# A graph layer's gathers: 45 tiles of rows move from the SP queue's single-row loads to POOL's indirect loads

## The chip, the cores and the metric

The kernel runs on one core of one Trainium2 chip. A core has five engines, each with an instruction queue of its own: TensorE (PE, matrix products; PEld is its weight load), VectorE (DVE), ScalarE (ACT), GpSimd (POOL) and SyncE (SP, which here issues transfers only). Sixteen DMA engines move data between device memory and the core's on-chip memory. The metric is the device time of one execution in microseconds (us).

## The reference

400,000 edges, sorted by destination, connect 12,500 nodes of 48 features. Each edge has 32 attributes. The layer is

```python
h = maximum(layernorm(x), 0)
tmp = concatenate([h[dst], h[src], edge_attr], axis=1)     # 400000 x 128
msg = relu(tmp @ W1 + b1) @ W2 + b2
out = x + segment_sum(msg, dst, num_segments=12500)
```

with W1 of 128 x 128 and W2 of 128 x 48, all float32.

## The kernel before

**Tables.** `tmp @ W1` splits into three products: one of the destination node, one of the source node, one of the edge. A first part of the kernel (about 135 us) computes for every node a row of 128 numbers for its use as destination (`tab_a`, bias included) and one for its use as source (`tab_b`), and writes both tables to device memory. The source table is also kept on chip, transposed, as `bt` (128 partitions, one column for each node).

**Chunks and steps.** The edges go in 3,125 tiles of P = 128 edges, and in NCH = 391 chunks of T = 8 tiles (the last has five). The loop at the end of `windows` takes one chunk further in each of 393 steps, in an order written out by hand: step c loads chunk c (`prepare`), multiplies chunk c-1 (`before`, `turned`, `hidden`) and sums chunk c-2 (`fold`, `add`). Because the edges are sorted, the 1,024 edges of a chunk point to a window of at most W = 80 destination nodes.

- `prepare(c)` has SP issue three loads: `rhs`, the 80 rows of `tab_a` that belong to the window (line 362; three buffers in turn), the edge attributes into the lower part of `lhs` (line 367), and the destinations, repeated over 80 partitions, into `row` (line 369). `lhs` and `row` have three buffers each. POOL issues the indirect loads of line 376: one for each tile, each fetching 128 rows of `tab_b` of 512 bytes into a slot of `gb`. There are six `gb` buffers, so the gathers of chunk c wait until line 420 has read chunk c-6. DVE compares `row` with the window's numbers (line 383) and builds the one-hot matrix `hot` (line 388).
- `before(c-1)` has PE compute `pre`, the destination part and the edge part in one product (line 401).
- `hidden(c-1)` has DVE add the gathered source rows `gb` to `pre` (line 420); ACT applies the relu (lines 424 and 425).
- `fold(c-2)` and `add(c-2)` sum a chunk's edges into its window by a product with `hot` (lines 433 and 438), and DVE adds that to a segment of 1,024 nodes (line 452) at a place that comes from a register.
- Every GQ = 12 chunks the segment changes (`segment_next`: lines 468 and 470). A finished segment is multiplied by W2 (lines 478 and 479), added to its part of x (line 480) and stored (line 484). SP issues the load of that part of x (line 461) and the store.

**Three ways to fetch source rows.** Most tiles are fetched by POOL's indirect loads. Two sets of tiles are not.

- `BYCOLS`, 361 chunks: the last tile of the chunk is copied out of `bt` on chip, one column of 128 x 1 for each edge, by DVE (59 columns in a step) and ACT (60) at line 353. Each copy has its place from a register; `load` fills these registers (line 304, TENSOR_LOAD). PE turns the finished tile and adds it to `pre` (line 411). The parts of a step's columns are spread over the step: 23, 20 and 16 on DVE and 28 and 32 on ACT.
- `BYROWS`, 45 chunks: one more tile of the chunk is fetched by SP, row by row, RPART = 15 rows in each step (`rows`, line 322), into a tile `gs` of its own. Each row takes a register number (sixteen of them in SP's load of line 304: the window's place and fifteen rows), a move and an issue. Line 420 then adds one tile less, and line 422 adds `gs` to the last one.

`last` is the table of these numbers, `WIDTH` = 140 for each step: up to 119 columns, the window's place at `BASE` = 120, fifteen rows, and four numbers for segments. A tile that is in neither set, or only in one, counts with POOL: `range(n - (c in BYCOLS) - (c in BYROWS))`, thus mostly seven gathers for a chunk, six where both sets have it, eight where none has.

Of the kernel before, what the change touches and what calls it, by code (L numbers as in the profile page):

```python
# [8 lines left out]
F32 = mybir.dt.float32  # L9
# [7 lines left out]
P = 128  # L17
N, D, DE, HID, E = 12500, 48, 32, 128, 400000
# [4 lines left out]
T = 8  # L23
# [20 lines left out]
U8 = mybir.dt.uint8  # L44
# [3 lines left out]


COLS = 1  # L50
ROWS0 = 1
END = NT // T


# [3 lines left out]
)  # L58
PART = sum(n for _, _, n, _ in PARTS)
BASE = 120  # L60
RPART = 15

BT0 = 16512
SEG0 = 122144
SEG_SIZE = 8 * L


SEG, NEXT, SEG2 = 136, 137, 138
PLACE0 = 139
WIDTH = 140  # L70
SLOTS = (NCH + 2 + P - 1) // P
MOST = 32

# [1 line left out]
def tiles_of(first, part):  # L75

    n = (END - first) * part // P
    return [first + (P * (j + 1) + part - 1) // part - 1 for j in range(n)]


BYCOLS = tiles_of(COLS, PART)
BYROWS = tiles_of(ROWS0, RPART)
EPS = 1e-5


# [149 lines left out]
def windows(nc, tc, gp, bt, ident, idx, x_t, tab_a, tab_b, dst, edge_t, w1, w2s, b2s, out_t):  # L235
# [3 lines left out]
    with ExitStack() as es:  # L239
# [5 lines left out]
        gtp = es.enter_context(tc.tile_pool(name="gtp", bufs=3))  # L245
# [13 lines left out]
        for _, _, n, at in PARTS:  # L259
# [1 line left out]
                last[:, :, at : at + n], last[:, :, at : at + n], 4, BT0,  # L261
                op0=ALU.mult, op1=ALU.add,
            )
        rows_at = slice(BASE, BASE + 1 + RPART)
        nc.vector.tensor_scalar(
            last[:, :, rows_at], last[:, :, rows_at], 4 * HID, None, op0=ALU.mult
        )
        tab8, taba8 = (t.rearrange("n h -> (n h)").bitcast(U8) for t in (tab_b, tab_a))

        place = PARTS[0][3] - 1  # L270
        for a, b in ((place, SEG2), (NEXT, SEG)):
# [5 lines left out]
        nc.vector.scalar_tensor_tensor(  # L277
            last[:, :, at_place], last[:, :, at_place], 4.0, last[:, :, PLACE0 : PLACE0 + 1],
            op0=ALU.mult, op1=ALU.add,
# [8 lines left out]
            rhss.append(rhs)  # L288
        st = {}
        gts = {}  # L290
        gss = {}

        def group(c):

            return divmod(c + OFF, GQ)
# [4 lines left out]
        def numbers(c, at, n, engine):  # L300

            got = []
            for k in range(0, n, MOST):
                got += nc.values_load_multi_w_load_instructions(  # L304
                    last[c % P : c % P + 1, c // P, at + k : at + min(k + MOST, n)],
                    engines=[engine], min_val=0, max_val=1 << 23,
                    skip_runtime_bounds_check_because="numbers of nodes, and what is made of them",
                )[1]
            return got

        def node(n):
            return n.with_bounds(min_val=0, max_val=N - 1)

        def rows(c, nodes):

            for k, n in enumerate(nodes):
                e = (c - ROWS0) * RPART + k
                of = BYROWS[e // P]
                if of not in gss:
                    gss[of] = gtp.tile([P, HID], F32, name="gs")  # L320
                n = n.with_bounds(min_val=0, max_val=4 * HID * (N - 1))
                nc.sync.dma_start(  # L322
                    gss[of].bitcast(U8)[e % P : e % P + 1, :],
                    tab8[bass.ds(n, 4 * HID)].rearrange("(o h) -> o h", o=1),
                )

        regs = {}

# [12 lines left out]
        def columns(c, part):  # L341

            dve, first, _, _ = PARTS[part]
            copy = nc.vector.tensor_copy if dve else nc.scalar.copy
            for k, at in enumerate(regs.pop((c, part), [])):
                j, e = divmod((c - COLS) * PART + first + k, P)
                of = BYCOLS[j]
                if of not in gts:
                    gts[of] = gtp.tile([HID, P], F32, name="gt")
                at = at.with_bounds(  # L350
                    min_val=BT0, max_val=BT0 + 4 * (N - 1), guaranteed_mod_val=0, out_of_modulus=4
                ) - BT0
                copy(gts[of][:, e : e + 1], bt8[:, bass.ds(at, 4)].bitcast(F32))  # L353

        def prepare(c):
            n = min(T, NT - c * T)
            at = c * CE
            m = max(0, min(RPART, len(BYROWS) * P - (c - ROWS0) * RPART)) if c >= ROWS0 else 0
            base, *nodes = numbers(c, BASE, 1 + m, mybir.EngineType.SP)
            rhs = rhss[c % 3]  # L360
            base = base.with_bounds(min_val=0, max_val=4 * HID * (N - 1))
            nc.sync.dma_start(
                rhs.bitcast(U8)[:W, :],
                taba8[bass.ds(base, 4 * HID * W)].rearrange("(w h) -> w h", w=W),
            )
            lhs = ld.tile([P, CE], F32, name="lhs")
            nc.sync.dma_start(lhs[W:K, : n * P], edge_t[:, at : at + n * P])
            row = ld.tile([W, CE], I16, name="row")
            nc.sync.dma_start(
                row[:, : n * P],  # L370
                dst[at : at + n * P].rearrange("(o e) -> o e", o=1).to_broadcast([W, n * P]),
            )
            st[c] = dict(n=n, rows=nodes)
            gb = gp.tile([P, T, HID], F32, name="gb")
            for t in range(n - (c in BYCOLS) - (c in BYROWS)):
                nc.gpsimd.indirect_dma_start(  # L376
                    out=gb[:, t, :], out_offset=None, in_=tab_b[:, :],
                    in_offset=bass.IndirectOffsetOnAxis(
                        ap=srci[:, c * T + t : c * T + t + 1], axis=0
                    ),  # L380
                )

            nc.vector.tensor_scalar(  # L383
                lhs[:W, : n * P], row[:, : n * P], bw[:, c : c + 1], None, op0=ALU.is_equal,
            )
            columns(c, 0)
            hot = wp.tile([P, T, W], F32, name="hot")
            nc.vector.tensor_tensor(  # L388
                hot[:, :n, :], wnum.unsqueeze(1).to_broadcast([P, n, W]),
                rel[:, c * T : c * T + n].unsqueeze(2).to_broadcast([P, n, W]), op=ALU.is_equal,  # L390
            )
            load(c, 1)
            st[c].update(rhs=rhs, lhs=lhs, gb=gb, hot=hot)
# [21 lines left out]
        def hidden(c):  # L415
            s = st[c]
            n, m, pre = s["n"], s["added"], s["pre"]
            h = wp.tile([P, T, HID], F32, name="hid")
            g = m - (c in BYROWS)
            nc.vector.tensor_add(h[:, :g, :], pre[:, :g, :], s["gb"][:, :g, :])  # L420
            if g < m:
                nc.vector.tensor_add(h[:, g, :], pre[:, g, :], gss.pop(c))
            if m < n:
                nc.scalar.activation(h[:, m, :], pre[:, m, :], AF.Relu)  # L424
            nc.scalar.activation(h[:, :m, :], h[:, :m, :], AF.Relu)  # L425
            s["h"] = h
# [16 lines left out]
        def add(c):  # L443

            s = st.pop(c)
            k = group(c)[0] % 2
            of = SEG0 + k * SEG_SIZE
            at = s["base"].with_bounds(
# [33 lines left out]
        def segment_store(g, n):  # L482
            first, = numbers(begin(g), SEG, 1, mybir.EngineType.SP)
            nc.sync.dma_start(out_t[:, bass.ds(node(first), n)], xs.pop(g)[:, :n])

        with tc.manual_schedule():
            for c in range(NCH + 2):
                if c < NCH:
                    prepare(c)
                    rows(c, st[c].pop("rows"))  # L490
                if c >= NCH:
                    columns(c, 0)
                columns(c, 1)
                load(c, 2)
                columns(c, 2)
                if 0 <= c - 1 < NCH:
                    before(c - 1)
                if 0 <= c - 2 < NCH:
                    fold(c - 2)
                if 0 <= c - 1 < NCH:  # L500
                    turned(c - 1)

                g, k = group(c - 2)
                if k == GQ - 3 or c == NCH - 1:
                    segment_load(g)
                if g > 0 and k < L // BLK:
                    segment_sum(g - 1, k, BLK)
                if g > 0 and k == STORE:
                    segment_store(g - 1, L)
                columns(c, 3)  # L510
                if 0 <= c - 1 < NCH:
                    hidden(c - 1)
                load(c + 1, 0)
                load(c, 4)
                columns(c, 4)
                if 0 <= c - 2 < NCH:
                    add(c - 2)
                    if k == GQ - 1:
                        segment_next(g)
                load(c + 1, 3)  # L520
                if c == NCH + 1:
                    segment_sum(g, 0, END_L)
                    segment_store(g, END_L)

                if c < PIECES:
                    s = slice(c * PIECE, (c + 1) * PIECE)
                    nc.sync.dma_start(out_t[:, s], x_t[:, s])
# [126 lines left out]
def tile_gnn_preln(  # L654
# [52 lines left out]
    flag = const.tile([1, 1], I32, name="flag")  # L707
    last = const.tile([P, SLOTS, WIDTH], I32, name="last")

# [157 lines left out]
```

## Time and profile before

| | |
|---|---|
| median of 3 runs | 5028.71 us (5015.86 to 5036.02) |
| the profiled execution | 5046.97 us |
| its span, first to last instruction | 5045.2 us |
| busy: PE, PEld | 3196.2 us (63%), 2891.6 us (57%) |
| busy: DVE, ACT, POOL | 2915.2 us (58%), 2927.7 us (58%), 2664.5 us (53%) |
| mean granted TensorE clock | 0.643 of full speed |
| DMA: software queue (POOL), hardware queue (SP, ACT) | 178.39 MB, 169.09 MB |
| mean DMA rate | 70 GB/s |

A group row reads: line, engine, operation, tiles written and read, shapes, count | busy time and mean duration of one in ns | idle time of the engine just before them, and what ended most of it ("issue" where the profile knows of nothing that the engine waited for). A row of the order of time reads: start, duration, engine, line, operation, and how many of a kind follow each other without a gap, with the idle time ahead in brackets; "SPq" is SP's queue, whose transfers are shown by their issue. A row of a stretch reads: from and to, length, and for each engine the busy time and, in brackets, the count; then the granted clock, the share of DMA time and GB/s. A row of the waits reads: who waited, for what, how long in total, how often, the longest.

### The profile page before, as it was taken

The numbers are of one execution on the slowest core, as the hardware profiler recorded it, in microseconds if no ns is written. First come the engines' busy times: TensorE is split into PE (matmuls) and PEld (weight loads), VectorE is DVE, ScalarE is ACT, GpSimd is POOL, SyncE is SP. The second block draws the span as 40 slices with busy tenths as digits, with TensorE's granted clock in tenths as the row PEclk, the third lists the DMA queues.
The fourth block names the chain that finished last, engine by engine and source line by source line (L and its number), as shares of the span: only waits on it lengthen the run. The fifth ranks groups of instructions, "written<-read, shape, count | busy, mean of one in ns | idle before, by whom it ended". The sixth has DMA issues, their size and how long they took to land. (4 is left out here: it accounts for less than half of the span.)

```text
span 5045.2 us, 105760 instructions
## 1 busy us (share of the span) xinstructions
PE 3196.2 (63%) x16917; PEld 2891.6 (57%) x16917; DVE 2915.2 (58%) x24786; ACT 2927.7 (58%) x24107; POOL 2664.5 (53%) x2746
## 2 busy tenths in 40 slices
PE   6565666665666665566666665666666666666676
PEld 4555555555555555556565555556555565555565
DVE  4555555555555555565555555555555565555555
ACT  3455655655555555566565555556565566555555
POOL 5455555555555555555555555555555555555553
PEclk8666666666666666666666666666666666665656
DMA  3422222222222222222222222222222222222221
GB/s 135 123 67 69 68 66 68 68 67 68 64 65 66 68 70 67 64 68 71 67 69 69 68 67 67 69 67 69 67 67 68 69 71 68 68 66 69 66 69 51
DMA packets 202255, 354.44 MB, mean 70 GB/s; under 512 B 70322, under 2 KB 108228, under 8 KB 200276
## 3 DMA queue, kind: packets, MB, share of 16 engines
q0 software_dynamic: 87040, 178.39, 14.2%
q1 hardware_dynamic: 114256, 169.09, 11.3%
q14 instruction: 560, 4.59, 0.3%
q8 instruction: 139, 2.28, 0.2%
q10 hardware_dynamic: 260, 0.10, 0.0%
HBM read 327.84 MB, written 22.07 MB: 69 GB/s over the span
## 5 line engine op out<-in xcount | busy, mean ns | idle before, releaser
L376 POOL DMA_INDIRECT gb<-tab_b,srci x2719 | 2643.0, 972 | 2315.4 <-DVE hid L420 1319.5
L353 ACT COPY gt<-bt 128x1 f32 x23280 | 2477.9, 189 | 1893.8 <-issue 1867.1
L353 DVE COPY gt<-bt 128x1 f32 x22928 | 1704.1, 143 | 1795.4 <-issue 1750.0
L433 PE MATMUL p_g<-hot,hid 128*128 128x80 f32 x6250 | 1392.9, 414 | 1664.1 <-ACT hid L425 1585.3
L433 PEld LDWEIGHTS p_g<-hot,hid 128*128 128x128 f32 x6250 | 1313.3, 320 | 1745.7 <-ACT hid L425 1689.4
L401 PEld LDWEIGHTS pre<-rhs,lhs 112*128 112x128 f32 x6250 | 1149.6, 283 | 92.8 <-issue 85.4
L401 PE MATMUL pre<-rhs,lhs 112*128 112x128 f32 x6250 | 1171.3, 366 | 17.1 <-DVE lhs L383 17.1
L420 DVE TENSOR_TENSOR hid<-pre,gb 128x896 f32<-128x896 f32 (+2 forms) x391 | 420.8, 1076 | 6.8 <-issue 4.4
L425 ACT ACTIVATE hid<-hid 128x896 f32<-128x896 f32 (+1 forms) x391 | 370.8, 948 | 39.3 <-DVE hid L420 38.0
L411 PE MATMUL pre<-ident,gt 128*128 128x128 f32 x722 | 278.7, 489 | 112.0 <-remote 104.9
L388 DVE TENSOR_TENSOR hot<-wnum,rel 128x640 f32<-128x640 f32 x391 | 315.9, 808 | 5.1 <-issue 4.9
L383 DVE TENSOR_SCALAR lhs<-row,bw 80x1024 f32<-80x1024 int16 x391 | 306.8, 785 | 12.8 <-DMA row<-in_dst 7.9
L438 PEld LDWEIGHTS <-ones 128*128 128x128 bf16 x3125 | 291.9, 154 | 0.0
L438 PE MATMUL p_g<-hot,ones 128*128 128x80 bf16 x3125 | 283.7, 265 | 0.0
L411 PEld LDWEIGHTS pre<-ident,gt 128*128 128x128 f32 x722 | 193.4, 328 | 118.4 <-remote 110.6
L452 DVE TENSOR_TENSOR seg<-seg,p_g 128x160 f32 x391 | 125.7, 321 | 191.8 <-DVE hid L420 156.8
L424 ACT ACTIVATE hid<-pre 128x128 f32<-128x128 f32 x361 | 97.5, 270 | 86.8 <-DVE hid L420 78.4
L478 PE MATMUL p_f<-seg,w2s 128*48 128x512 f32 (+1 forms) x134 | 121.0, 1005 | 0.4 <-DVE seg L452 0.4
L479 PE MATMUL p_f<-seg,b2s 1*48 1x512 f32 (+1 forms) x134 | 95.5, 801 | 0.0
L479 PEld LDWEIGHTS p_f<-seg,b2s 1*48 1x48 f32 x134 | 13.1, 143 | 100.8 <-issue 100.8
L468 DVE MEMSET seg<- 128x944 f32 x64 | 54.1, 845 | 9.5 <-issue 0.3
L480 DVE TENSOR_TENSOR xseg<-xseg,p_f 48x512 f32<-48x512 f32 (+1 forms) x67 | 44.8, 668 | 23.3 <-PE p_f L479 22.4
(67 smaller groups left out, 306.3 us busy)
## 6 DMA issues: line engine op xcount, KB each, us to landing
gs<-tab_b SPq DMA_DIRECT2D x5760, 0.5 KB
row<-in_dst SPq DMA_DIRECT2D x390, 160.0 KB
lhs<-in_edge_t SPq DMA_DIRECT2D x390, 128.0 KB
gb<-tab_b,srci POOLq DMA_INDIRECT x2719
rhs<-tab_a SPq DMA_DIRECT2D x391, 40.0 KB
xseg<-in_x_t SPq DMA_DIRECT2D x33, 192.0 KB
out_x<-xseg SPq DMA_DIRECT2D x33, 192.0 KB
tab_b<-tab SPq DMA_DIRECT2D x3, 1280.0 KB
```

Source lines behind the costliest of these rows:

```text
L353: copy(gts[of][:, e : e + 1], bt8[:, bass.ds(at, 4)].bitcast(F32))
L376: nc.gpsimd.indirect_dma_start(out=gb[:, t, :], out_offset=None, in_=tab_b[:, :], in_offset=bass.IndirectOffsetOnAxis(ap=srci[:, c * T + t ...
L383: nc.vector.tensor_scalar(lhs[:W, : n * P], row[:, : n * P], bw[:, c : c + 1], None, op0=ALU.is_equal,)
L388: nc.vector.tensor_tensor(hot[:, :n, :], wnum.unsqueeze(1).to_broadcast([P, n, W]), rel[:, c * T : c * T + n].unsqueeze(2).to_broadcast([P ...
L401: nc.tensor.matmul(pre[:, t, :], s["lhs"][:K, t * P : (t + 1) * P], s["rhs"][:K, :], start=True, stop=c not in BYCOLS or t < n - 1,)
L411: nc.tensor.matmul(s["pre"][:, s["n"] - 1, :], gts.pop(c), ident, start=False, stop=True)
L420: nc.vector.tensor_add(h[:, :g, :], pre[:, :g, :], s["gb"][:, :g, :])
L425: nc.scalar.activation(h[:, :m, :], h[:, :m, :], AF.Relu)
L433: nc.tensor.matmul(p_g[:, 0, :], s["h"][:, t, :], s["hot"][:, t, :], start=t == 0, stop=t == n - 1)
L438: nc.tensor.matmul(p_g[:, 1, :], ones, high[:, t, 1::2], start=t == 0, stop=t == n - 1)
L452: nc.vector.tensor_add(to, to, s["p_g"])
L478: nc.tensor.matmul(p_f[:, :n], w2s, seg[:, 0, s], start=True, stop=False)
```

## The change

The set `BYROWS` and all that serves it go. Its 45 tiles are fetched as the others are, by one more indirect load of POOL each, into a slot of `gb`; line 420 adds all gathered tiles of a chunk at once and line 422 goes. SP's register load holds one number, and what SP issues for a chunk are the three loads of `prepare`. The number table shrinks from 140 to 125 columns, and with it the fixed SBUF place of the segments moves by 224 bytes. Sizes, buffers and the order of all else stay.

```diff
-ROWS0 = 1
...
-RPART = 15
...
-SEG0 = 122144
+SEG0 = 121920
...
-SEG, NEXT, SEG2 = 136, 137, 138
-PLACE0 = 139
-WIDTH = 140
+SEG, NEXT, SEG2 = 121, 122, 123
+PLACE0 = 124
+WIDTH = 125
...
-BYROWS = tiles_of(ROWS0, RPART)
...
-        rows_at = slice(BASE, BASE + 1 + RPART)
+        rows_at = slice(BASE, BASE + 1)
...
-        def rows(c, nodes):
-
-            for k, n in enumerate(nodes):
-                e = (c - ROWS0) * RPART + k
-                of = BYROWS[e // P]
-                if of not in gss:
-                    gss[of] = gtp.tile([P, HID], F32, name="gs")
-                n = n.with_bounds(min_val=0, max_val=4 * HID * (N - 1))
-                nc.sync.dma_start(
-                    gss[of].bitcast(U8)[e % P : e % P + 1, :],
-                    tab8[bass.ds(n, 4 * HID)].rearrange("(o h) -> o h", o=1),
-                )
...
         def prepare(c):
             n = min(T, NT - c * T)
             at = c * CE
-            m = max(0, min(RPART, len(BYROWS) * P - (c - ROWS0) * RPART)) if c >= ROWS0 else 0
-            base, *nodes = numbers(c, BASE, 1 + m, mybir.EngineType.SP)
+            base, = numbers(c, BASE, 1, mybir.EngineType.SP)
...
-            for t in range(n - (c in BYCOLS) - (c in BYROWS)):
+            for t in range(n - (c in BYCOLS)):
                 nc.gpsimd.indirect_dma_start(
...
-            g = m - (c in BYROWS)
-            nc.vector.tensor_add(h[:, :g, :], pre[:, :g, :], s["gb"][:, :g, :])
-            if g < m:
-                nc.vector.tensor_add(h[:, g, :], pre[:, g, :], gss.pop(c))
+            nc.vector.tensor_add(h[:, :m, :], pre[:, :m, :], s["gb"][:, :m, :])
...
                 if c < NCH:
                     prepare(c)
-                    rows(c, st[c].pop("rows"))
```

More of the change, by code (lines that the diff above doesn't have):

```diff
@@ L267, in windows @@
         )
-        tab8, taba8 = (t.rearrange("n h -> (n h)").bitcast(U8) for t in (tab_b, tab_a))
+        taba8 = tab_a.rearrange("n h -> (n h)").bitcast(U8)
         place = PARTS[0][3] - 1
@@ L290, in windows @@
         gts = {}
-        gss = {}
         def group(c):
@@ L372, in prepare @@
             )
-            st[c] = dict(n=n, rows=nodes)
+            st[c] = dict(n=n)
             gb = gp.tile([P, T, HID], F32, name="gb")
-            for t in range(n - (c in BYCOLS) - (c in BYROWS)):
+            for t in range(n - (c in BYCOLS)):
                 nc.gpsimd.indirect_dma_start(
@@ L827 @@
         numbers[COLS : COLS + len(cols), at : at + n] = cols[:, k : k + n]
-    in_rows = np.array(BYROWS) * T + T - 1 - np.isin(BYROWS, BYCOLS)
-    rows = by_tile[in_rows].reshape(-1)
-    rows = np.pad(rows, (0, -len(rows) % RPART)).reshape(-1, RPART)
-    numbers[ROWS0 : ROWS0 + len(rows), BASE + 1 : BASE + 1 + RPART] = rows
     last = np.ascontiguousarray(numbers.reshape(SLOTS, P, WIDTH).transpose(1, 0, 2))
```

## The prediction

> **What bounds the kernel now.** I read the page first, then the groups by line with shapes kept apart, the waits, and last the order of time inside single steps.
>
> ```profile
> span 5045.2 us, 105760 instructions
> ...
> L376 POOL DMA_INDIRECT gb<-tab_b,srci x2719 | 2643.0, 972 | 2315.4 <-DVE hid L420 1319.5 <-issue 710.5 <-DVE hid L422 165.9
> L353 DVE COPY gt<-bt 128x1 f32 x22928 | 1704.1, 143 | 1795.4 <-issue 1750.0 <-DMA gb<-tab_b,srci 1.7
> L420 DVE TENSOR_TENSOR hid<-pre,gb 128x896 f32<-128x896 f32 x328 | 355.1, 1083 | 6.0 <-issue 4.4 <-PE pre L411 0.6
> L420 DVE TENSOR_TENSOR hid<-pre,gb 128x768 f32<-128x768 f32 x39 | 37.0, 948 | 0.8 <-PE pre L411 0.7
> L422 DVE TENSOR_TENSOR hid<-pre,gs 128x128 f32<-128x128 f32 x45 | 12.6, 280 | 0.0
> ```
>
> No engine is busy for much over 60% of the span. POOL's idle time ends on the addition of line 420, which frees a gb buffer; DVE loses 1750 us ahead of its single-column copies, where the profile knows no releaser. The step, from one addition of line 420 to the next, shows how the two belong together:
>
> ```profile
> core 0: us, PE busy (x) PEld busy (x) DVE busy (x) ACT busy (x) POOL busy (x), PEclk, DMA share, GB/s
> 919.16:931.20 12.04, 7.54 (x42) 7.35 (x42) 7.12 (x65) 7.12 (x60) 6.97 (x7) 0.72 0.32 84
> 943.62:954.28 10.66, 7.21 (x42) 7.02 (x42) 6.75 (x65) 6.86 (x59) 5.95 (x6) 0.68 0.26 71
> 981.50:994.80 13.30, 7.13 (x42) 6.94 (x42) 7.01 (x64) 7.29 (x60) 8.07 (x8) 0.68 0.30 83
> 968.71:981.50 12.79, 8.95 (x51) 5.86 (x49) 7.62 (x66) 6.06 (x48) 6.62 (x7) 0.84 0.24 63
> 1279.30:1291.54 12.24, 11.86 (x46) 8.07 (x45) 7.80 (x65) 5.89 (x47) 6.62 (x7) 0.50 0.15 40
> 1434.36:1446.55 12.19, 10.23 (x48) 6.93 (x47) 7.73 (x65) 6.05 (x50) 6.62 (x7) 0.61 0.15 39
> 4957.07:4969.55 12.48, 8.19 (x42) 7.96 (x42) 6.91 (x64) 7.74 (x69) 6.82 (x7) 0.60 0.35 93
> 4969.55:4981.66 12.11, 5.52 (x35) 5.08 (x34) 6.84 (x65) 7.52 (x65) 6.89 (x7) 0.64 0.30 83
> 5000.29:5007.87 7.58, 5.87 (x54) 5.48 (x53) 6.47 (x65) 6.50 (x61) 0.00 (x0) 0.99 0.14 40
> ```
>
> The length of a step follows POOL's count: 10.66 us with six gathers, 12.04 with seven, 13.30 with eight, and 7.58 once POOL has nothing left, although DVE and ACT do the same work. Of the 391 additions
>
> ```profile
> 158.51 1.22 DVE L420 TENSOR_TENSOR hid<-pre,gb 128x1024 f32<-128x1024 f32 x1
> ...
> 5032.55 0.81 DVE L420 TENSOR_TENSOR hid<-pre,gb 128x640 f32<-128x640 f32 x1
> ```
>
> I take the 379 steps between the fourth (196.25) and the one at 4957.07: 39 with six gathers last 11.38 us on average, 319 with seven 12.63, 21 with eight 13.64. So POOL waits for DVE, and DVE crawls while POOL gathers. How it crawls:
>
> ```profile
> 975.74 0.22 DVE L353 COPY gt<-bt 128x1 f32 x2 [1.20 <-issue]
> 976.46 0.15 DVE L353 COPY gt<-bt 128x1 f32 x1 [0.51 <-issue]
> ...
> 980.05 0.94 DVE L353 COPY gt<-bt 128x1 f32 x14 [0.55 <-issue]
> ```
>
> ```profile
> 975.73 0.28 ACT L353 COPY gt<-bt 128x1 f32 x2 [1.13 <-issue]
> ```
>
> DVE gets one or two copies through at a time, 0.72 us apart (975.74, 976.46), and ACT gets its own at the same instant (975.73). The release comes at 980.05, 1.54 us after POOL's seventh gather ended (row below: 977.56 + 0.95). Then DVE runs off fourteen copies and line 420 follows.
>
> ```profile
> 977.56 0.95 POOL L376 DMA_INDIRECT gb<-tab_b,srci  x1 [0.31 <-issue]
> ```
>
> SP works through it as well: fifteen single rows, here from 971.04, last 9.97 us, 0.66 each, where the seven from 4955.24, at the end of a crawl, took 0.39 each.
>
> ```profile
> 971.04 9.97 SPq L322 DMA_DIRECT2D gs<-tab_b  x15
> ...
> 1269.80 8.32 SPq L322 DMA_DIRECT2D gs<-tab_b  x15
> ...
> 1291.64 0.35 SPq L484 DMA_DIRECT2D out_x<-xseg  x1
> ...
> 4955.24 2.73 SPq L322 DMA_DIRECT2D gs<-tab_b  x7
> ```
>
> **The change part by part.** *Gathers added.* Each of the 45 tiles that SP filled row by row (45 x 128 = 5760 issues) becomes one more DMA_INDIRECT on POOL: 2764 for 2719. Each costs 0.95 us and the 0.30 us of issue behind it. Cover would have to come from POOL's 1319.5 us of waiting for line 420; but that wait is the other half of the loop, not slack. Of the 45, 39 make a six into a seven (12.63 - 11.38 = 1.25 us each, 49 us) and six a seven into an eight (13.64 - 12.63 = 1.01, 6 us). Sum +55 us. If POOL's wait covered them after all, they would cost 0; the averages speak against it.
>
> *The second addition removed.* Line 422 goes 45 times, and line 420 is 128x896 where it was 128x768. Busy time: 948 + 280 - 1083 = 145 ns, 6.5 us in all; the two overlap in the pipeline, so between 0 and -6.5; I take -3.
>
> *SP's rows removed.* 5760 issues, as many register moves, and fifteen of sixteen numbers in each of SP's register loads. The transfers only change queues, since the gathers fetch the same 5760 rows. SP itself was not late:
>
> ```profile
> DVE lhs L383 <- DMA row<-in_dst: 7.9, 1, 7.9
> ```
>
> is all that DVE ever waited for SP's loads by name, so SP's own time is worth nothing on the path. What may be worth something is the beat. In seven steps with seven gathers SP issued no row while the copies crawled: five times it stood in its queue for a store (from 1278.12 to 1291.64 in the rows above, and the like four more times), and twice its rows were at an end (after 4957.97). Copies within 4.00 to 11.24 us of the step (stretch, its length, busy time and count on DVE, the same on ACT, granted clock, DMA share and GB/s):
>
> ```profile
> 972.71:979.95 7.24, 1.99 (x22) 2.73 (x23) 0.76 0.23 59
> 1283.30:1290.54 7.24, 2.72 (x31) 3.16 (x29) 0.50 0.21 55
> 1438.36:1445.60 7.24, 2.78 (x35) 3.38 (x33) 0.63 0.21 57
> 4961.55:4968.79 7.24, 1.95 (x24) 2.86 (x26) 0.50 0.41 106
> 4973.55:4980.79 7.24, 1.98 (x25) 3.56 (x31) 0.50 0.27 76
> ```
>
> The first row is a step with SP at work (22 copies on DVE), the others have SP at rest. Over all seven (the first is the step 1279.30, the last 4969.55) the mean is 29.9, over the 314 others with seven gathers 25.0. Per crawl the three queues look like sharers of one supply: without SP, the other two get more. 4.9 copies at 0.06 us (fourteen in 0.94 us at 980.05, the 0.14 of a last one taken off, thirteen steps) are 0.29 us, which no longer follow the release. The lengths agree: 12.31 us over the seven, 12.63 over all 319, a gain of 0.32. But five of the seven are of one kind, the step after a change of segment, which had no loads in flight either; the two others (12.48, 12.11) stand 0.09 us below the 12.39 that the 263 steps away from the change average. The ends are thus 0.09 and, if every step shrank to the 12.19 to 12.24 of the rest steps, 0.42 us. I take 0.24, three quarters of 0.32, nearer to the counts than to the two last rows because counts and beat show the same sharing in both kinds: 379 x 0.24 = -91 us (ends -34 and -159).
>
> *The rest.* Shorter index table, SBUF places moved, first loads not behind rows: within the 7.9 us above, taken as 0.
>
> Sum: +55 - 3 - 91 = -39 us. The profiled execution took 5046.97 us (span 5045.2 and 1.8 around it), 18.3 above the median of 5028.71; -39 makes it 5008, and against the median **4990 us**.
>
> **The rivals.** *Nothing is returned (slower).* The copies crawl because POOL gathers, whoever else issues; then +55 - 3 = +52 us, 5081. For it: the two steps at 4957 and 4969, SP silent, are barely shorter, and their 24 and 25 copies are the ordinary 25.0. Against it: 31 and 35. It decides as soon as the return is under 52 / 379 = 0.137 us a step, and it sits in the 45 steps that gain a gather. [...]
>
> *All steps fall to the rest length.* 0.42 us a step: +55 - 3 - 159 = -107, 4922. For it: five steps within 0.54 us of each other. Against it: those had no loads moving (DMA share 0.15 against 0.24), and the changed kernel keeps the three loads.
>
> *The change does not do what it says*, because SP's order still holds segment loads and stores: SP stands at the store of line 484 as now,
>
> ```profile
> SPq L484 <- DVE xseg L480: 117.8, 24, 27.8
> ```
>
> with loads two steps ahead. That is no loss; it only makes more of the steps at rest, and goes with the forecast, 4990.
>
> **How the numbers follow.** Forecast (return of 0.15 to 0.36 a step) 0.55, own range 4945 to 5025; nothing or too little returned 0.31; full return 0.14. The range reaches to the two rivals: 4910 to 5085. A measurement of this kernel tells about 0.5% (25 us) from no change. Faster by more needs a return over 0.2 us: two thirds of the forecast and all of the full return, 0.50. Within 0.5%: the rest of the forecast, 0.17. Slower: 0.33.
>
> **What would show it.** Steps with seven gathers at about 12.39 us on average, where they were 12.63 (more of them near 12.1), and 28 or more copies in the 7.24 us window: the sharing is right. No steps with six gathers, 27 with eight at about 13.4: the price of a gather is right. DVE's idle time before line 353 falls from 1750 us to about 1715 (55 more for the gathers, 91 less). Wrong: seven-gather steps still at 12.5 to 12.6 with 25 copies (then 5081), or POOL's waiting down by 57 us with the span unchanged (then the gathers were covered).

## The result, and the profile after

| | before | changed |
|---|---|---|
| median of 4 runs each | 5032.36 us (5015.86 to 5038.81) | 6382.51 us (6382.25 to 6383.16) |
| span of the profiled execution | 5045.2 us | 6380.5 us |

The changed kernel takes 1.269 times as long (95% interval 1.266 to 1.272). The forecast was 4990 us.

The page of the changed kernel: the span, the busy tenths in 40 slices of it, and the groups that answer to those shown of before.

```profile
span 6380.5 us, 94216 instructions
...
PE 3296.0 (52%) x16917; PEld 2966.1 (46%) x16917; DVE 2786.1 (44%) x24741; ACT 2783.2 (44%) x24107; POOL 2686.2 (42%) x2791
...
DVE  4555556655533333333333333333333333333333
ACT  3556655566533333333333333333333333333333
...
L358 POOL DMA_INDIRECT gb<-tab_b,srci x2764 | 2664.7, 964 | 3599.0 <-DVE hid L401 2845.5
L336 ACT COPY gt<-bt 128x1 f32 x23280 | 2338.1, 187 | 3418.5 <-issue 3400.3
...
L336 DVE COPY gt<-bt 128x1 f32 x22928 | 1569.6, 142 | 2245.3 <-issue 2213.9
...
L431 DVE TENSOR_TENSOR seg<-seg,p_g 128x160 f32 x391 | 125.7, 322 | 1211.6 <-issue 1143.9
L401 DVE TENSOR_TENSOR hid<-pre,gb 128x896 f32<-128x896 f32 (+1 forms) x391 | 426.3, 1090 | 3.1 <-issue 1.2
```

Line numbers have moved: the gathers are line 358 now, the column copies 336, the addition that ends a step 401, the sum into the segment 431, the register loads 300. Apart from PE and PEld, whose clock was lower for most of the span (0.59 in the second stretch below), and POOL with its 45 gathers, no engine is busy for longer than before. DVE's copies lose 2245.3 us where they lost 1795.4, DVE loses another 1211.6 us ahead of line 431 where it was 191.8 ahead of line 452 (row below, of before), and POOL waits 2845.5 us for line 401 where it was 1319.5 for line 420. And the slices change once: up to the eleventh of 40 (1755 us) DVE and ACT are busy for five or six tenths, from there on for three to the end.

```profile
L452 DVE TENSOR_TENSOR seg<-seg,p_g 128x160 f32 x391 | 125.7, 321 | 191.8 <-DVE hid L420 156.8
```

The additions that end a step, counted in two stretches of each kernel (from and to, length, busy time and count, then clock, DMA share and GB/s). Before:

```profile
core 0: us, DVE busy (x), PEclk, DMA share, GB/s
196.00:1749.50 1553.50, 132.34 (x123) 0.64 0.25 68
1749.50:4957.00 3207.50, 275.47 (x256) 0.64 0.26 68
```

After:

```profile
core 0: us, DVE busy (x), PEclk, DMA share, GB/s
195.00:1716.90 1521.90, 134.06 (x123) 0.64 0.26 68
1717.00:6293.00 4576.00, 282.34 (x259) 0.59 0.18 48
```

The same first 123 steps take 1521.9 us in place of 1553.5: 12.37 a step, where before had 12.63. The changed kernel is 32 us ahead at 1717 us. Then a step takes 4576 / 259 = 17.67 us, where before has 3207.5 / 256 = 12.53. From there to the end the changed kernel needs 6380.5 - 1717.0 = 4663.5 us, before 5045.2 - 1749.5 = 3295.7: 1368 us lost, against 32 won.

The order of time on DVE around that point, in the changed kernel (in brackets the idle time ahead):

```profile
1713.34 0.28 DVE L336 COPY gt<-bt 128x1 f32 x3 [1.16 <-issue]
1714.08 0.15 DVE L336 COPY gt<-bt 128x1 f32 x1 [0.46 <-issue]
...
1717.02 1.08 DVE L401 TENSOR_TENSOR hid<-pre,gb 128x896 f32<-128x896 f32 x1
1723.15 0.32 DVE L431 TENSOR_TENSOR seg<-seg,p_g 128x160 f32 x1 [5.05 <-issue]
...
1724.05 1.67 DVE L336 COPY gt<-bt 128x1 f32 x23
...
1729.48 1.30 DVE L336 COPY gt<-bt 128x1 f32 x20 [2.42 <-issue]
1733.77 1.06 DVE L336 COPY gt<-bt 128x1 f32 x16 [2.99 <-issue]
1734.75 1.08 DVE L401 TENSOR_TENSOR hid<-pre,gb 128x896 f32<-128x896 f32 x1
```

Up to 1717 the crawl is there, one to three copies at a time. After it the copies run in whole parts of 23, 20 and 16, each at one go, and the idle time stands ahead of the parts. What stands ahead of a part is its register load: one of 4.50 us starts at 1724.89 and ends 0.09 us ahead of the twenty copies at 1729.48. The loads of line 300 (instances, then shortest, median and longest in ns), first between 300 and 1700 us, then between 1800 and 6300:

```profile
L300 DVEq TENSOR_LOAD <-last x349: 307/1382/2380, 301.0 to 1696.0; - x175
L300 ACTq TENSOR_LOAD <-last x227: 1717/1911/2454, 299.6 to 1697.0; - x114
L300 SPq TENSOR_LOAD <-last x131: 267/275/478, 307.0 to 1691.5; - x131
...
L300 DVEq TENSOR_LOAD <-last x784: 309/4618/6312, 1799.5 to 6299.1; - x196
L300 ACTq TENSOR_LOAD <-last x509: 5954/6261/7164, 1798.4 to 6297.5; - x170
L300 SPq TENSOR_LOAD <-last x298: 262/273/480, 1800.2 to 6299.5; - x149
```

The same loads of the same numbers of registers take 3.3 times as long. DVE's three loads of a step have 24 (the 23 columns of the first part and the place in the segment), 20 and 16 registers, so its median is a load of 20: 69 ns a register, then 231. SP's load of one register stays at some 0.27 us, although its place in blocks 1 to 3 is no multiple of 16 bytes either. In before, the loads of this second stretch are the short ones:

```profile
L304 DVEq TENSOR_LOAD <-last x764: 307/1382/2095, 1798.9 to 4898.1; - x191
```

What changes at that step is the place of the numbers. `last` holds step c in partition c mod 128 at block c div 128, and a block is `WIDTH` numbers of 4 bytes. With 140 the blocks begin at 0, 560, 1120 and 1680 bytes, multiples of 16 all; with 125 at 0, 500, 1000 and 1500, of which only the first is one. The parts begin at numbers 0, 24, 44, 60 and 88 of a block, at multiples of 16 bytes in themselves. Block 1 begins with step 128, whose loads run ahead of its sums, just where the time jumps.

### The profile page after: what moved, and what is told of

Its sections match the earlier page's. It is cut to its first block, busy times and chain, and to the rows that moved or that the text cites. A ratio compares the mean times of both kernels' runs of the same rounds, so it can differ in the third digit from the quotient of the medians.

```text
span 6380.5 us, 94216 instructions
## 1 busy us (share of the span) xinstructions
PE 3296.0 (52%) x16917; PEld 2966.1 (46%) x16917; DVE 2786.1 (44%) x24741; ACT 2783.2 (44%) x24107; POOL 2686.2 (42%) x2791
## 4 chain that ended last, share of the span: by engine, by line
issue 53%; DVE 32%; POOL 6%; DVEq 4%; PE 2%; ACT 2%; another core or an unknown queue 1%; DMA 1%; SPq 0%; ACTq 0%; POOLq 0%
DVE gt L336 18%; POOL gb L358 6%; DVE hid L401 5%; DVE lhs L365 4%; DVEq L300 4%; DVE hot L370 4%; ACT gt L336 1%; DVE seg L431 1%; PE p_n L178 1%; PE p_g L412 0%; DVE seg L447 0%; DVE xseg L459 0%; PE p_n L199 0%; PE pre L383 0%
## 5 line engine op out<-in xcount | busy, mean ns | idle before, releaser
L358 POOL DMA_INDIRECT gb<-tab_b,srci x2764 | 2664.7, 964 | 3599.0 <-DVE hid L401 2845.5
L336 ACT COPY gt<-bt 128x1 f32 x23280 | 2338.1, 187 | 3418.5 <-issue 3400.3
L412 PE MATMUL p_g<-hot,hid 128*128 128x80 f32 x6250 | 1426.1, 422 | 2810.3 <-ACT hid L404 2650.3
L412 PEld LDWEIGHTS p_g<-hot,hid 128*128 128x128 f32 x6250 | 1342.7, 326 | 2897.4 <-ACT hid L404 2730.0
L336 DVE COPY gt<-bt 128x1 f32 x22928 | 1569.6, 142 | 2245.3 <-issue 2213.9
L383 PEld LDWEIGHTS pre<-rhs,lhs 112*128 112x128 f32 x6250 | 1186.0, 291 | 101.3 <-issue 89.6
L383 PE MATMUL pre<-rhs,lhs 112*128 112x128 f32 x6250 | 1209.8, 375 | 16.9 <-DVE lhs L365 16.8
L431 DVE TENSOR_TENSOR seg<-seg,p_g 128x160 f32 x391 | 125.7, 322 | 1211.6 <-issue 1143.9
L401 DVE TENSOR_TENSOR hid<-pre,gb 128x896 f32<-128x896 f32 (+1 forms) x391 | 426.3, 1090 | 3.1 <-issue 1.2
```

Of the source, the lines that this page charges most:

```text
L358: nc.gpsimd.indirect_dma_start(out=gb[:, t, :], out_offset=None, in_=tab_b[:, :], in_offset=bass.IndirectOffsetOnAxis(ap=srci[:, c * T + t ...
L383: nc.tensor.matmul(pre[:, t, :], s["lhs"][:K, t * P : (t + 1) * P], s["rhs"][:K, :], start=True, stop=c not in BYCOLS or t < n - 1,)
L401: nc.vector.tensor_add(h[:, :m, :], pre[:, :m, :], s["gb"][:, :m, :])
L412: nc.tensor.matmul(p_g[:, 0, :], s["h"][:, t, :], s["hot"][:, t, :], start=t == 0, stop=t == n - 1)
L431: nc.vector.tensor_add(to, to, s["p_g"])
```

## The experiments

The theory: here a load of 16 or more registers whose first number does not stand at a multiple of 16 bytes of the table costs 3.3 times as much (4.62 us for 1.38). The rivals: it is the shorter table, or the segments' moved place, or SP's missing rows.

**The width alone, both ways.** The changed kernel with 128 numbers a step (512 bytes), and the kernel before with 141 (564 bytes). The segments' place moves along by 32 bytes, as the table grows.

```diff
-SEG0 = 121920
+SEG0 = 121952
...
-WIDTH = 125
+WIDTH = 128
```

> The changed kernel with three unused numbers added to each row of the number table: 128 numbers wide instead of 125, so that the second, third and fourth block of 128 steps begin at 512, 1024 and 1536 bytes in place of 500, 1000 and 1500. Theory (place of the numbers): the jump from 12.4 to 17.7 us a step at step 126 is the register loads, which take 0.065 us a register where they begin at a multiple of 16 bytes and 0.22 us where they do not; then all steps keep the 12.37 us of the first 122 and the run takes 4910 to 5000 us, below the kernel before. Rival (a freed SP that stands at its waits, or loads that run ahead, bring the core into a slower state after some 1700 us): 6380 us again, jump and all.

```diff
-SEG0 = 122144
+SEG0 = 122176
...
-WIDTH = 140
+WIDTH = 141
```

> The kernel before, single rows and all, with one unused number added to each row of the table: 141 wide, so the later blocks begin at 564, 1128 and 1692 bytes. Place of the numbers: 12.6 us a step up to step 126, then 17.5 us or more (SP's load of sixteen numbers is slow too), 6300 to 6600 us in all. Rival (it takes the removal of SP's rows): 5030 us.

Measured, on one chip where the kernel before takes 4972.1 us: the changed kernel 128 wide takes 4901.14 us (6 runs), 0.986 of before (interval 0.983 to 0.989), and the kernel before 141 wide 6403.47 us (one run). The first is 9 us under the range that the theory gave, the second within it. The changed kernel at 128, its steps in the same two stretches and its loads:

```profile
195.00:1717.00 1522.00, 136.33 (x125) 0.63 0.26 70
1717.00:4800.00 3083.00, 276.15 (x253) 0.65 0.26 70
...
L300 DVEq TENSOR_LOAD <-last x379: 304/1382/2086, 1901.2 to 3396.6; - x190
L300 ACTq TENSOR_LOAD <-last x247: 1709/1938/2497, 1899.1 to 3397.7; - x124
```

12.18 us a step before the point and 12.19 behind it: no jump. The kernel before at 141, DVE's slices and its loads early and late:

```profile
DVE  4556555556533333333333333333333333333333
...
L304 DVEq TENSOR_LOAD <-last x219: 308/1382/2384, 302.9 to 1194.5; - x110
...
L304 DVEq TENSOR_LOAD <-last x261: 311/4621/6314, 1899.7 to 3396.3; - x131
```

It has SP's rows and a longer table, and yet falls to three tenths at the same step, with the same 4.62 us. That excludes the shorter table and the missing rows: the width makes the loss, and three more numbers a step take it back. The segments' place moved along with the width in both runs, so these two do not exclude it; the run that is 126 wide, below, keeps that place.

**One engine's loads alone.** Wide tables, every block aligned, and of the columns' parts only those of one engine begin 4 bytes past a multiple of 16, in all blocks. The numbers behind the columns, which are loaded singly, move along. First ACT's:

```diff
-    (False, 59, 28, 60), (False, 87, 32, 88),
+    (False, 59, 28, 61), (False, 87, 32, 89),
...
-WIDTH = 125
+WIDTH = 128
```

> The changed kernel at 128 numbers, with ACT's two groups of numbers alone one place further on, 4 bytes past a multiple of 16, from the first step. Place of the numbers: ACT's loads of 28 and 32 registers take 6.2 and 7.1 us from the start, DVE's stay at 1.1 to 1.7. ACT's own sequence after the jump (copies 3.3 and 2.7, relu 1.1, two waits of 5.0 and 5.2) adds up to 17.2 us, so it can set the step alone: 6700 to 7000 us. If DVE's loads set the step and ACT's only follow: 5000 us.

Then DVE's, with ACT's parts at 64 and 92:

```diff
-    (True, 0, 23, 1), (True, 23, 20, 24), (True, 43, 16, 44),
+    (True, 0, 23, 2), (True, 23, 20, 25), (True, 43, 16, 45),
...
-WIDTH = 125
+WIDTH = 132
```

> The same with DVE's three groups alone one place further on and ACT's at multiples of 16 (132 numbers wide). Place of the numbers: DVE's loads of 24, 20 and 16 registers take 5.5, 4.6 and 3.7 us, ACT's stay at 1.8 and 2.0. DVE's sequence after the jump (7.1 us of work, waits of 4.4, 3.3 and 3.1) adds up to 17.9 us: 6900 to 7100 us. If ACT's loads set the step: 5000 us.

Measured: 7087.23 us and 7061.78 us, one run each. Both are slow from the first step; ACT's is 87 us over its range, DVE's within. With ACT's off, the loads and the addition:

```profile
L300 DVEq TENSOR_LOAD <-last x262: 307/1382/2422, 1900.0 to 3395.9; - x131
L300 ACTq TENSOR_LOAD <-last x169: 5964/6801/7120, 1899.3 to 3390.7; - x169
...
L401 DVE TENSOR_TENSOR hid<-pre,gb 128x896 f32<-128x896 f32 (+1 forms) x391 | 429.2, 1098 | 2161.1 <-PE pre L393 1579.9
```

With DVE's off:

```profile
L300 DVEq TENSOR_LOAD <-last x262: 310/4616/6324, 1898.8 to 3398.8; - x131
L300 ACTq TENSOR_LOAD <-last x170: 1717/1917/2508, 1900.0 to 3391.3; - x170
...
L401 DVE TENSOR_TENSOR hid<-pre,gb 128x896 f32<-128x896 f32 (+1 forms) x391 | 426.5, 1091 | 4.5 <-issue 1.9
```

Only the misplaced engine's loads are long, and either engine alone is enough: where ACT is late, DVE's addition waits for line 393, the turning of the columns that ACT copies; where DVE is late, it waits for nobody. The two engines load side by side, about 13.9 us a step on DVE (3 x 4.62) and about 13 on ACT (two loads of 6.0 to 7.1). From the fourth addition on a step lasts 17.8 us with ACT's off alone and 17.7 with DVE's off alone, as it does with both off (17.7), so mending one of them would have brought almost nothing. The remaining 4 us of a 17.67 us step would be the issue of some 60 copies and what else stands in the same queue; that is argued, not shown.

**How many bytes.** The changed kernel 126 wide, with all other places of SBUF as they were: the blocks begin at 0, 504 = 31.5 x 16, 1008 = 63 x 16 and 1512 = 94.5 x 16 bytes.

```diff
-WIDTH = 125
+WIDTH = 126
```

> The changed kernel at 126 numbers, all SBUF places as in the changed kernel: the blocks of 128 steps begin at 504 bytes (8 past a multiple of 16), 1008 (a multiple of 16, not of 32) and 1512 (8 past). If 16 bytes are what counts: steps up to 126 and from 254 to 382 at 12.3 us, those between at 17.5; 5500 to 5650 us. If 8 bytes were enough: 4900 us. If 32 or 64 were needed: slow from 126 to the end, 6380 us, as it also would be if something in the run, and not the place, started the slow steps.

Measured: 4738.06 us, on another chip, where the kernel before takes 3570.14 us (below); the expectation in us was made for the slower kind. DVE's slices, and the additions in blocks 0, 1 and 2:

```profile
DVE  5888777777533333333333333333358887777773
...
195.00:1272.00 1077.00, 131.01 (x120) 0.75 0.35 94
1275.00:3500.00 2225.00, 137.31 (x126) 0.59 0.18 48
3507.00:4610.00 1103.00, 138.01 (x126) 0.77 0.35 95
```

8.98, 17.66 and 8.75 us a step: block 2 is as quick as block 0, so neither the segments' place, which is that of the changed kernel, nor something that builds up in the run makes the slow steps. Its 1008 bytes are a multiple of 16 and not of 32, block 1's 504 is one of 8 and not of 16; DVE's loads have a median of 1.38 us in block 0 and 4.62 us in block 1. So for these loads a multiple of 16 bytes is enough and one of 8 is not. The slow step is 17.7 us on this chip too, for the loads set it.

**The other terms: gathers and rows.** The kernel before with POOL's 45 gathers added and SP's rows kept (140 wide) gives the price of the gathers:

```diff
-            for t in range(n - (c in BYCOLS) - (c in BYROWS)):
+            for t in range(n - (c in BYCOLS)):
...
-            g = m - (c in BYROWS)
-            nc.vector.tensor_add(h[:, :g, :], pre[:, :g, :], s["gb"][:, :g, :])
-            if g < m:
-                nc.vector.tensor_add(h[:, g, :], pre[:, g, :], gss.pop(c))
+            if c in BYROWS:
+                nc.vector.tensor_copy(h[:, m - 1, :1], gss.pop(c)[:, :1])
+            nc.vector.tensor_add(h[:, :m, :], pre[:, :m, :], s["gb"][:, :m, :])
```

> The kernel before with the 45 gathers added to POOL and SP's 5760 single rows kept (the rows are fetched, and one column of them is copied to a place that the addition of line 420 then overwrites; 140 numbers wide). It prices the gathers alone. The prediction's term: 55 us more than the kernel before, about 1.1%, with no step of six gathers left. If POOL's waiting covers them: no difference.

The changed kernel, 128 wide, without the 45 gathers (their source rows are missing from its sums) gives what SP's silence returns:

```diff
+LEFT = tiles_of(1, 15)
...
-            for t in range(n - (c in BYCOLS)):
+            for t in range(n - (c in BYCOLS) - (c in LEFT)):
...
-            nc.vector.tensor_add(h[:, :m, :], pre[:, :m, :], s["gb"][:, :m, :])
+            g = m - (c in LEFT)
+            nc.vector.tensor_add(h[:, :g, :], pre[:, :g, :], s["gb"][:, :g, :])
+            if g < m:
+                nc.vector.tensor_copy(h[:, g, :], pre[:, g, :])
```

> The changed kernel at 128 numbers with the 45 gathers left out as well: the source rows of these 45 tiles are not added, a copy of pre takes the place of line 422. It prices the removal of SP's rows alone. The prediction's term: 91 us less than the kernel before (0.24 us a step), its ends 34 and 159. With the 71 us by which the kernel at 128 numbers is faster and 55 us for the gathers it would be 126 us less, 2.5%. If SP's rows are worth nothing: no difference from the kernel before.

They were run on the chip of the 126-wide run, where the kernel before takes 3570.14 us: 3622.34 us with the gathers added, ratio 1.014 (1.012 to 1.016), and 3572.93 us without rows and gathers, ratio 1.0007 (0.9995 to 1.0018). So 52.2 / 45 = 1.16 us for a gather, and nothing returned. The return that had left the 128-wide kernel 71 us ahead on the chip of the width experiments, gathers paid, was not there on this one. The changed kernel at 128 was then put beside the two on one chip:

> The changed kernel with the table 128 numbers wide again, beside the two that follow on one chip. So far it was 71 us faster than the kernel before (ratio 0.986) on a chip where the kernel before takes 4972 us, and never ran where the kernel before takes 3570 us. Theory, that what the removal of SP's rows returns hangs on the chip's pace: where the kernel before takes about 5000 us, 4830 to 4930 us in ratio 0.98 to 0.99 again; where it takes about 3570 us, nothing is returned and the 45 gathers are paid, 3615 to 3630 us, ratio 1.013 to 1.017. Rival, that the return does not hang on the chip: ratio 0.98 to 0.99 on both, 3500 to 3535 us on the second kind.

> The changed kernel, 128 wide, with the 45 added gathers left out as well: their source rows are missing from the sums, so the output lacks them. It holds the return alone. Theory: where the kernel before takes about 5000 us, some 71 us of gain seen plus 52 to 55 us of gathers, so 115 to 135 us below the kernel before, ratio 0.973 to 0.977; where it takes about 3570 us, the same as the kernel before within 0.2%. Rival, that most of the 71 us came from the 128-wide table itself and not from SP's rows: this run would show the same return, and only the next one, which keeps both rows and table, would stand below 45 times the price of a gather.

> The kernel before with POOL's 45 gathers added and SP's rows kept (table 140 wide). It holds the price of the gathers alone. The forecast's term is 55 us: ratio 1.010 to 1.012 where the kernel before takes about 5000 us (5020 to 5085 us), and 1.012 to 1.016 where it takes about 3570 us, as measured there. If a gather in a step where the copies pass slowly costs less than in the forecast because the copies and not POOL set the step, the time is within 0.5% of the kernel before.

It was another chip of this quicker kind: before 3568.87 us; the changed kernel at 128 3630.06 us, ratio 1.017 (1.015 to 1.019); without rows and gathers 3574.63, 1.002 (1.0005 to 1.0029); with both 3621.73, 1.015 (1.013 to 1.017). All three fall where the theory put them for a chip of this kind (the first at the upper edge, 3630 us). The 61.2 us lost are 52.9 for the gathers and 5.8 for the rows' removal, and 2.5 left. The chain of waits by engine and two groups of the changed kernel at 128 on this chip:

```profile
POOL 56%; issue 27%; DVE 7%; DMA 6%; PE 2%; DVEq 1%; ACT 1%; ACTq 0%; POOLq 0%; SPq 0%
...
L358 POOL DMA_INDIRECT gb<-tab_b,srci x2764 | 2709.5, 980 | 875.3 <-issue 808.3
...
L336 DVE COPY gt<-bt 128x1 f32 x22928 | 1497.8, 142 | 261.9 <-issue 219.9
```

and the copies of the kernel with rows and gathers there:

```profile
L353 DVE COPY gt<-bt 128x1 f32 x22928 | 1497.9, 142 | 263.6 <-issue 221.9
```

POOL runs on without waiting for line 401, its gathers set the pace, and DVE's copies lose 262 us over the whole span where before had lost 1795.4 in the profiled execution of the prediction. They do so with SP's rows (263.6) and without them (261.9): there is no crawl on this chip, and nothing that SP's silence could return. One more pair was tried:

> Once more the kernel of the return alone (128 wide, neither SP's rows nor the 45 gathers, whose source rows are missing from the output), for a chip where the kernel before takes about 5000 us; twice it ran where that takes 3570 us. Theory: the gain of 71 us that the kernel with the gathers had there plus the price of the gathers, so 110 to 135 us below the kernel before, ratio 0.973 to 0.978, steps of seven gathers or fewer at about 12.1 us. Where the kernel before takes about 3570 us: the same within 0.3%, as twice before.

> Once more the price of the 45 gathers alone, beside the kernel above, for a chip where the kernel before takes about 5000 us. The forecast's term: 55 us, ratio 1.010 to 1.012. If the copies that pass slowly set the step and not the gathers, within 0.5% of the kernel before. Where that takes about 3570 us: ratio 1.013 to 1.016, as twice before.

One more chip of the quicker kind: before 3569.45 us, without rows and gathers 3572.43 (1.0012, interval 1.0002 to 1.0022), with both 3625.73 (1.016, 1.015 to 1.018; 1.25 us a gather). On a chip with the crawl neither term was therefore measured by itself.

## Why the prediction was wrong

- *"The rest. Shorter index table, SBUF places moved, ... taken as 0."* This is the step that failed. The working bounded it by what DVE waits for SP's transfers by name, 7.9 us (two waits for single rows add 4.3); the register loads stand in no such row, and it never asked what a load itself costs at another place. The table's width puts three of four blocks off the 16 bytes, and that costs 5.14 us (17.67 - 12.53) in each step from the 127th on, 1368 us in all. No rival of the prediction held it, and neither did its range. The loads' durations were in the trace, three a step on DVE with a median of 1.38 us, and had no part in the working. With the blocks aligned, on the chip of the width experiments, the change is 71 us faster than before, where the working had 39 (own range 4 to 84 below its median of 5028.71).
- *Gathers added, +55 us.* Right in kind and size, as far as it was measured: 52.2, 52.9 and 56.3 us on three chips, without the crawl. There are no steps with six gathers any more. In the aligned stretch of the changed kernel eight gathers last 13.22 us on average and seven 12.31, so 0.91 for the step from one to the other, where the forecast had 1.01.
- *SP's rows removed, -91 us.* Where the copies crawl, the runs agree with the mechanism, and its size was too small; no run there takes the rows away and leaves all else. In the first 123 steps, all in block 0, seven gathers (103 steps before, 114 after) fall from 12.73 to 12.31 us and eight (7 and 9) from 13.50 to 13.22, and the 13 steps with six are gone; so 15 of the added gathers stand there (13 x 1.25 + 2 x 1.01 = 18 us) and yet the steps are 32 us shorter in all, which makes (32 + 18) / 123 = 0.41 us a step returned, the forecast's upper end (0.42) and not its 0.24. DVE starts 27.7 copies between 4.00 and 11.24 us of a seven-gather step, where the same steps before start 23.6. The chip of the width experiments repeats it: in the same 123 steps, with both tables aligned there, the kernel with the rows (141 wide) takes 1535.0 us and the one without them (128 wide) 1496.4, although that one has the 15 gathers more; seven gathers fall from 12.58 to 12.10 us. There the whole is 71 us; with 52 to 56 us for the gathers, a price taken from chips without the crawl, that is 123 to 127 us, or about 0.33 a step, an estimate. The share taken off for the two rows that stood low (three quarters of 0.32) was caution in the wrong direction.
- *The rival "nothing is returned".* On the three chips without the crawl it is what the runs show: the rows' removal returns nothing, and on the one of them where the whole change ran at an aligned width it was 61 us slower, where the rival had 52. The prediction had one chip's trace and could not see this.
- *The signs named beforehand.* Twenty-seven steps with eight gathers: seen. Seven gathers at 12.39: 12.31 in block 0, not behind it. Twenty-eight copies in the window: 28.8 in block 0, counted as the prediction counts them, with those that reach into it (25.0 before). DVE's idle time ahead of the copies, for which no releaser is known, at 1715: 2213.9, and 1528.2 in the 128-wide kernel, whose row shows that the copies did get more of their time back:

```profile
L336 DVE COPY gt<-bt 128x1 f32 x22928 | 1698.3, 143 | 1614.3 <-issue 1528.2
```

## What to carry to other kernels

Where many registers are loaded at once from a table, let every load begin at a multiple of 16 bytes (here 20 registers took 1.38 us there, and 4.62 us at 4 or 8 bytes past it): pad the row's width to a multiple of four numbers and begin each part of it at one. An edit that shortens a shared table or moves its fields is not free because fewer numbers are read; work out the new byte address of each thing that is loaded from it, in every block and not only in the first. And before a gain is counted on that comes from one engine's silence, see whether the stall it relieves is there on more than one chip: here the same edit at an aligned width was 1.4% faster on one and 1.7% slower on another.

## What the runs showed of the hardware

- DVE's and ACT's loads of 16 to 32 registers were quick only where their first number stood at a multiple of 16 bytes, counted from the table's start. Aligned, DVE's loads of 16, 20 and 24 registers take 1.12, 1.38 and 1.64 us (medians of before, behind 1800 us), 65 ns for each register more. Misaligned, they take 3.71, 4.62 and 5.53 us (blocks 1 and 2 of the changed kernel, 4 and 8 bytes past), 227 ns for each register more. ACT's loads of 28 and 32 registers take 1.70 to 2.82 us in the one case and 5.95 to 7.16 in the other (the same kernels, behind 1800 us). SP's single register takes 0.27 us in either case. Why a misaligned load takes longer was not shown.
- The crawl of the copies goes with the chip, or with the occasion: each chip was used once. The kernel before takes 4972.1 us on the chip of the width experiments (5032.36 where it was first compared) and 3570.14, 3568.87 and 3569.45 us on three others, where DVE's copies run through while POOL gathers. What differs between these chips, and why the copies crawl on some, was not found and stays open.
